# Layer 2's transposes and layer 3's RMS factors by transfers, bias rows and loop blocks added by transfers from GpSimd

## The chip, the cores and the metric

The kernel runs on one core of one Trainium2 chip. The metric is the device time of one execution in microseconds (us). The engines are named as the profile names them: PE is TensorE (PEld its weight loads), DVE is VectorE, ACT is ScalarE, POOL is GpSimd, SP is SyncE, which here only issues transfers.

## What is computed

Thirty-two graphs of 512 nodes pass through four layers. Each graph has node features x (512 x 256) and an adjacency adj (512 x 512), all in float32, and each layer is followed by a residual sum and a layer norm:

```python
# layer 0: GIN
h = (1.0 + eps) * x + adj @ x
x = layernorm(x + (relu(h @ W1 + b1) @ W2 + b2))            # hidden 512
# layer 1: GCN
h = adj @ (x @ W.T + b)
x = layernorm(x + where(h > 0, h, alpha * h))
# layer 2: a layer norm of its own, then a graph convolution
h = layer_norm(x, gamma, beta)
x = layernorm(x + (x + relu((adj @ h) @ W_rel + b_rel + h @ W_root)))
# layer 3: GIN with an RMS norm
h = (eps * x + adj @ x) @ W1 + b1                            # hidden 1024
x = layernorm(x + (silu(h * rsqrt(mean(h * h) + 1e-6) * w) @ W2 + b2))
```

## The kernel before

**Products by seven.** Every large product is a Strassen-Winograd scheme (`seven`, lines 583 to 599): operands are cut into 2 x 2 blocks, sums of blocks are formed on VectorE (`left_sums`, `right_sums`), and seven block products stand for eight. Weights get their sums once, the adjacency gets its sums once per graph (`Adjacency.sums`, line 650), features at each use. `aggregate` (line 685) forms adj @ x transposed, with features on partitions; `dense_feat` (line 725) multiplies by a weight and stays feature-major; `dense_add` (line 768) returns to token-major and adds into a tile that already holds the residual; `dense_tok` (line 713) is layer 1's plain product. A graph has 106 matmuls of 256 columns, 112 of 128 columns and 12 transposes on TensorE. A float32 matmul leaves two records in the trace, a transpose one.

**Where the change touches.**
- *Loops.* The factors (1 + eps) of layer 0 and eps of layer 3 lie on the diagonal of the adjacency. Four diagonal blocks, in the adjacency's two halves and in two of its sums (`self.loops`, line 655), are saved before layer 0 (`kept`, four transfers within SBUF, lines 659 to 665), get a scaled identity added on VectorE (`with_loops`, line 671: four additions of 128x256), are restored after layer 0 (`restore`, line 667: four transfers) and get another identity added after layer 2 (line 951).
- *Bias rows.* `plus_row` (line 874) adds a 256-wide bias to a 512 x 256 tile in four additions on GpSimd, in layer 0 (line 901) and layer 3 (line 958). The evictions of `dense_add` then add to that tile.
- *Layer 2's transposes.* h is token-major and is needed feature-major too: eight TensorE transposes of 128 x 128 into two PSUM banks and two copies out (lines 938 to 943).
- *RMS factors.* Layer 3 squares h, sums it over features (`column_sums`, line 793: one transposing reduction and three small additions on VectorE leave 32 partitions x 4 sums for each quarter), scales the sums in four small instructions, takes the power -1/2 on GpSimd (`inv_sqrt`, line 513, 128 x 4), and spreads each token's factor to all partitions by four transposes of a broadcast column into PSUM (lines 971 to 977). VectorE multiplies hT by that PSUM bank (line 981), ScalarE takes silu, VectorE forms sums, and the second dense product follows.

**What sets the order.** The whole program is written out by a planner (`Plan`, lines 191 to 403). Every operation is recorded with its engine (some may go to ScalarE or VectorE), a cost from formulas (lines 36 to 80), and what it must wait for. `order` (line 317) then plays all engines forward, each with one queue in order, and picks on each the ready operation with the lowest rank; ranks come from the graph's number times a period plus how much TensorE work of that graph lies ahead. `RULES` (line 95) lists the sets of period and pace tried; the one that ends first in the planner's reckoning is written out. Four graphs may be in flight (`FLIGHT`, line 444); they share 36 SBUF tiles of 128 x 1024 (`rooms`), 12 small tiles and 8 PSUM banks, and a graph further back must leave some free (`spare`). All transfers are issued by SP in that order (`move`, line 276), reckoned at 0.45 us of SP (`ISSUE`), 1.5 us, the bytes and 0.35 us to land; eight are in flight at most (`LANES`). GpSimd has the bias additions and the powers. All instructions come from one helper line (L266), transfers from L280.

Of the kernel before, what the change touches and what calls it, by code (L numbers as in the profile page):

```python
# [26 lines left out]


def in_psum(x):
    return isinstance(x, Part) and x.room.pool.psum  # L30
# [35 lines left out]
def gpsimd_time(n):  # L66
    return 0.15 + n * 0.0024, 0.05


# [6 lines left out]
ISSUE, ADVANCE, AFTER, LANES = 0.45, 1.5, 0.35, 8  # L76
# [18 lines left out]
RULES = [(50, 2, last, near) for last in (12, 20) for near in (0, 0.5, 1)]  # L95


class Pool:


    def __init__(self, tiles, grain, spare, psum):
        self.tiles, self.grain, self.spare, self.psum = tiles, grain, spare, psum
        self.clear()

    def clear(self):
        self.rooms = [None] * len(self.tiles)

    def free(self):

        return sorted(  # L110
            (0.0 if r is None else r.until, i)
            for i, r in enumerate(self.rooms)
            if r is None or not r.left
        )


class Room:


    def __init__(self, pool):  # L120
        self.pool = pool
        self.uses = 0
        self.clear()

    def clear(self):
        self.index = None
        self.left = self.uses
        self.until = 0.0


class Part:
# [34 lines left out]
    def place(self):  # L166
        v = self.room.pool.tiles[self.room.index]
        for step in self.steps:
            v = step(v)
        return v  # L170
# [3 lines left out]
class Op:  # L174

    graph: int
    rank: tuple
    ways: dict  # L180
    port: set
# [9 lines left out]
class Plan:  # L191
# [10 lines left out]
    def grains(self, x):  # L202
        part = isinstance(x, Part)
# [4 lines left out]
        for step, n in dims[:-1]:  # L208
            starts = [s + step * i for s in starts for i in range(n)] if step else starts
        step, n = dims[-1]  # L210
        return {
            (key, g)
            for s in starts
            for g in range(s // grain, (s + step * (n - 1)) // grain + 1)
        }

    def add(self, ways, out, ins, ordered=None, port=(), kbytes=0):
        me = len(self.ops)
        op = Op(self.graph, (self.graph, me), ways, port, "scalar" in ways, kbytes)
        self.ops.append(op)  # L220
        before, results = set(), set()
        writes = self.grains(out) if out is not None else set()
# [22 lines left out]
    def do(self, out, *ways, ordered=None, scrap=None):  # L245
# [3 lines left out]
        port = set()  # L249
        for e, method, _, args, kw in ways:  # L250
            tiles = [x for x in (*args, *kw.values()) if isinstance(x, (bass.AP, Part))]
            ins += tiles
            if e == "gpsimd" and kw.get("op") != ALU.pow or e == "vector" and not (
                method.startswith("bn_") or any(in_psum(x) for x in tiles)
            ):
                port.add(e)

        def issue(engine, method, args, kw):
# [14 lines left out]
            out, ins, ordered, port,  # L273
        )

    def move(self, out, src, kbytes, inward=True):


        def issue():
            self.nc.sync.dma_start(*(x.place() if isinstance(x, Part) else x for x in (out, src)))  # L280

        self.add(
            {"sync": ((ISSUE, ADVANCE + wire_time(kbytes) + AFTER), issue)},
            out if inward else None, [src] if isinstance(src, Part) else [], kbytes=kbytes,
        )
# [31 lines left out]
    def order(self, period, pace, last, near):  # L317
# [15 lines left out]
        oldest, port, wire, lanes = 0, 0.0, 0.0, [0.0] * LANES  # L333
        can_start = {i for i, n in enumerate(behind) if not n}
        done = []
        while can_start:
# [4 lines left out]
            def rooms_free(op):  # L341

                count = {}
                for r in op.rooms:
                    if r.index is None:
                        count[r.pool] = count.get(r.pool, 0) + 1
                at = 0.0
                for pool, n in count.items():
                    if pool not in room_at:
                        room_at[pool] = pool.free()  # L350
                    n += pool.spare[min(op.graph - oldest, len(pool.spare) - 1)]
                    if op.graph - oldest >= self.flight or n > len(room_at[pool]):
                        return None
                    at = max(at, room_at[pool][n - 1][0])
# [3 lines left out]
            for i in can_start:  # L358
# [4 lines left out]
                if op.kbytes:  # L363
                    wait = max(wait, lanes[0])
                at = {
                    e: max(free[e], wait, ready[i][e], port if e in op.port else 0.0)
                    for e in op.ways
                }
                way = min(at, key=lambda e: at[e] + sum(op.ways[e][0]) + (YIELD if op.yields and e == "vector" else 0.0))
# [11 lines left out]
            if op.kbytes:  # L381
                wire = max(wire, t + ADVANCE) + wire_time(op.kbytes)
                end = wire + AFTER
                lanes = [*lanes[1:], end]
            if engine in op.port:
                port = end
            for r in op.rooms:
                if r.index is None:
                    r.index = r.pool.free()[0][1]
                    r.pool.rooms[r.index] = r  # L390
# [16 lines left out]
def tile_gnn_stack(ctx: ExitStack, tc: tile.TileContext, a: dict, out: bass.AP):  # L407
# [36 lines left out]
    FLIGHT, ROOMS, SMALL = 4, 36, 12  # L444
# [3 lines left out]
    psum = ctx.enter_context(tc.tile_pool(name="psum", bufs=1, space=bass.MemoryType.PSUM))  # L448
    plan = Plan(nc, FLIGHT)

    def pool(kind, name, n, size, grain, spare):
        return Pool(
            [kind.tile([P, size], F32, tag=f"{name}{i}", name=f"{name}{i}") for i in range(n)],
            grain, spare, kind is psum,
# [3 lines left out]
    rooms = pool(work, "room", ROOMS, NC * D, P, (0, 4, 6, 8))  # L458
# [5 lines left out]

    def gpsimd(method, n, *args, **kw):
        return "gpsimd", method, gpsimd_time(n), args, kw
# [22 lines left out]
    def both(method, o, x, y, engines):  # L489
        plan.do(o, *(e(method, span(o), x, y) for e in engines))  # L490

    def add(o, x, y, *engines):
        both("tensor_add", o, x, y, engines or (vector,))

    def sub(o, x, y, *engines):
        both("tensor_sub", o, x, y, engines or (vector,))

    def mul(o, x, y):
        both("tensor_mul", o, x, y, (vector,))
# [10 lines left out]
    def carry(o, x):  # L510
        plan.move(o, x, P * span(o) / 256)

    def inv_sqrt(o, x):
        n = span(o)
        plan.do(
            o, ("gpsimd", "tensor_tensor", power_time(n), (x, mhalf[:, 0:n]), dict(op=ALU.pow))
# [3 lines left out]
    def room(*shape):  # L520
        return Part(Room(rooms)).shaped(*shape)

# [54 lines left out]
    mhalf = constant("mhalf", [P, 2 * NC])  # L577
# [56 lines left out]
    class Adjacency:  # L634
# [15 lines left out]
        def sums(self):  # L650
# [8 lines left out]
            kept = room(4, HC, P)  # L659
            self.plain = [kept[:, i] for i in range(4)]  # L660
            for d, o in zip(self.plain, self.loops):
                if plan.graph:
                    carry(d, o)
                else:
                    copy(d, o)

        def restore(self):
            for d, o in zip(self.plain, self.loops):
                carry(o, d)

        def with_loops(self, loop):
            for d, o in zip(self.plain, self.loops):
                add(o, d, loop.unsqueeze(1).to_broadcast(list(o.shape)), vector)

        def row_sums(self):

            rows = room(N)
# [79 lines left out]
    def dense_sums(upper, lower):  # L757
# [3 lines left out]
        for pairs in zip(upper, lower):  # L761
            blocks = [x[:, :, j * TH : (j + 1) * TH] for x in pairs for j in range(2)]
            sums = right_sums(*blocks, [room(2, TH) for _ in range(3)], blocks[1])
# [29 lines left out]
    def column_sums(t, put):  # L793
# [3 lines left out]
        few = small(16)  # L797
# [7 lines left out]
        for q in range(1, P // Q):  # L805
            add(few[0:Q], few[0:Q], few[q * Q : (q + 1) * Q])
        for q in range(P // Q):
            put(slice(q * Q, (q + 1) * Q), few[0:Q, q :: P // Q])
# [64 lines left out]

    def plus_row(x, r):

        for c in range(NC):
            add(x[:, c, :], x[:, c, :], r, gpsimd)
# [31 lines left out]
    def layer1(x, adjacency):  # L909
# [4 lines left out]
        column_sums(rows, lambda p, sums: ts(rs[p], sums, 1.0, None, ALU.mult))  # L914
# [20 lines left out]
    def layer2(h, xx, u, adjacency):  # L935

        aT = aggregate(h, adjacency)
        hT = Wide(DC)
        for j in range(DC):
            ps = bank(N)  # L940
            for c in range(NC):
# [144 lines left out]
```

## Time and profile before

| | |
|---|---|
| median of 3 runs | 2364.99 us (2363.84 to 2365.42) |
| profiled execution: time, span, mean granted clock | 2366.02 us, 2364.2 us, 0.997 |
| PE: busy, instructions | 2330.0 us (99%), 14362 |
| DVE: busy, instructions | 2138.4 us (90%), 5485 |
| ACT: busy, instructions | 1570.1 us (66%), 3994 |
| POOL: busy, instructions | 407.7 us (17%), 422 |
| additions of loop blocks on DVE | 256 x 416 ns = 103.9 us |
| additions of bias rows on POOL | 256 x 769 ns = 194.6 us |
| powers on POOL, 4 and 8 columns | 128 x 1243 ns, 32 x 1672 ns |
| transfers within SBUF | 252 of 128 KB, 2.2 us from issue to landing |
| packets of SP's queue | 103280, 14.5% of 16 engines' span |

How it is read: *busy* is the union of an engine's records and the share is of the span. In a group's line, "line engine op out<-in" come first, then shapes and count, then busy time, the mean of one, and the idle time of that engine just before with what ended most of it. In a table by stretches, each line has the stretch, its length, then each engine's busy time with the number of instructions in brackets, then TensorE's granted clock (1.00 is full), the busy share of the transfer engines and GB/s. Matmuls are pipelined, so their records overlap: the mean of one record is longer than the time from one start to the next. The last chain is followed back from the last instruction, at each step to what released it.

### The profile page before, as it was taken

The numbers are of one execution on the slowest core, as the hardware profiler recorded it, in microseconds if no ns is written. First come the engines' busy times: TensorE is split into PE (matmuls) and PEld (weight loads), VectorE is DVE, ScalarE is ACT, GpSimd is POOL, SyncE is SP. The second block draws the span as 40 slices with busy tenths as digits, with TensorE's granted clock in tenths as the row PEclk, the third lists the DMA queues.
The fourth block names the chain that finished last, engine by engine and source line by source line (L and its number), as shares of the span: only waits on it lengthen the run. The fifth ranks groups of instructions, "written<-read, shape, count | busy, mean of one in ns | idle before, by whom it ended". The sixth has DMA issues, their size and how long they took to land.

```text
span 2364.2 us, 40948 instructions
## 1 busy us (share of the span) xinstructions
PE 2330.0 (99%) x14362; PEld 2135.4 (90%) x14362; DVE 2138.4 (90%) x5485; ACT 1570.1 (66%) x3994; POOL 407.7 (17%) x422
## 2 busy tenths in 40 slices
PE   8999999999999999999999999999999999989997
PEld 7899989999999999999999999999999989978997
DVE  6899989999999999999999999999999999988997
ACT  3767666667666676766676666776666766565764
POOL 1112111111121121111111211111111112111111
PEclk9999999999999999999999999999999999999999
DMA  7001110111110111101111101111011111011000
GB/s 218 12 8 54 50 54 12 52 50 51 53 35 30 50 54 50 54 14 50 50 52 52 44 20 50 54 50 54 14 50 50 52 52 46 23 52 48 10 10 28
DMA packets 103487, 107.25 MB, mean 45 GB/s; under 512 B 10865, under 2 KB 78193, under 8 KB 103281
## 3 DMA queue, kind: packets, MB, share of 16 engines
q1 hardware_dynamic: 103280, 104.64, 14.5%
q8 instruction: 113, 1.85, 0.3%
q14 instruction: 94, 0.76, 0.1%
HBM read 54.80 MB, written 16.78 MB: 30 GB/s over the span
## 4 chain that ended last, share of the span: by engine, by line
PE 91%; DVE 4%; DMA 2%; ACT 1%; issue 1%; SPq 0%; POOL 0%; POOLq 0%; ACTq 0%; DVEq 0%
PE ps L266 91%; DVE room L266 3%; ACT room L266 1%; DVE few L266 1%; DMA room<-in_x_dram 1%; ACT scrap L266 1%; DMA room<-room 1%; SPq L280 0%; DMA L_gnn_eps<-in_L_gnn_eps_dram 0%; DMA room<-in_adj_dram 0%; POOL few L266 0%; ACT L266 0%; POOLq L1082 0%; DVE L_gnn_W L266 0%; DVE A L266 0%
## 5 line engine op out<-in xcount | busy, mean ns | idle before, releaser
L266 PE MATMUL ps<-room,room 128*128 128x256 f32 x3584 | 911.9, 380 | 9.8 <-DMA room<-in_x_dram 5.8
L266 DVE TENSOR_TENSOR room<-ps,room 128x256 f32<-128x256 f32 (+1 forms) x1344 | 629.6, 475 | 149.3 <-PE ps L266 122.6
L266 PEld LDWEIGHTS ps<-room,room 128*128 128x128 f32 x3584 | 650.1, 191 | 88.8 <-issue 7.1
L266 DVE TENSOR_TENSOR room<-room,room 128x512 f32<-128x512 f32 (+1 forms) x1120 | 640.6, 585 | 9.9 <-ACT room L266 3.1
L266 PE MATMUL ps<-L_gnn_W,room 128*128 128x128 f32 (+1 forms) x3584 | 622.7, 291 | 7.2 <-ACT room L266 4.9
L266 PEld LDWEIGHTS ps<-L_gnn_W,room 128*128 128x128 f32 x3584 | 525.3, 192 | 31.1 <-ACT room L266 7.2
L266 PE MATMUL ps<-A,room 128*128 128x128 f32 x3072 | 489.2, 276 | 1.8 <-ACT room L266 1.1
L266 PEld LDWEIGHTS ps<-A,room 128*128 128x128 f32 x3072 | 434.8, 192 | 15.8 <-ACT room L266 1.3
L266 PE MATMUL ps<-room,L_gnn_W 128*128 128x256 f32 x1536 | 424.6, 380 | 1.0 <-DVE room L266 0.9
L266 ACT ACTIVATE room<-ps,L_gnn_b_c 128x256 f32<-128x256 f32 x768 | 318.2, 472 | 157.2 <-PE ps L266 157.0
L266 POOL TENSOR_TENSOR few<-few,mhalf 128x4 f32<-128x4 f32 (+1 forms) x160 | 212.5, 1329 | 1211.0 <-DVE few L266 1208.5
L266 ACT ACTIVATE room<-ps 128x256 f32<-128x256 f32 (+1 forms) x546 | 215.0, 407 | 298.5 <-PE ps L266 294.7
L266 ACT ACTIVATE room<-room,few 128x256 f32<-128x256 f32 x624 | 341.0, 603 | 107.0 <-DVE few L266 103.7
L266 DVE TENSOR_TENSOR room<-room 128x256 f32<-128x256 f32 (+1 forms) x640 | 330.4, 518 | 18.0 <-DMA room<-in_adj_dram 5.7
L266 POOL TENSOR_TENSOR room<-room,L_gnn_b 128x256 f32<-128x256 f32 x256 | 194.6, 769 | 739.6 <-PE ps L266 519.0
L266 PE MATMUL ps<-room,A 128*128 128x256 f32 x1152 | 319.2, 380 | 3.0 <-ACT room L266 3.0
L266 PEld LDWEIGHTS ps<-room,L_gnn_W 128*128 128x128 f32 x1536 | 279.7, 191 | 33.1 <-DVE room L266 2.2
L266 ACT ACTIVATE room<-room 128x1024 f32<-128x1024 f32 (+2 forms) x260 | 245.8, 946 | 18.1 <-DVE room L266 16.5
L266 ACT ACTIVATE room<-room,L_gnn_rms_weight_c 128x512 f32<-128x512 f32 x256 | 179.7, 718 | 111.3 <-DVE room L266 108.2
L266 PEld LDWEIGHTS ps<-room,A 128*128 128x128 f32 x1152 | 206.5, 191 | 27.1 <-ACT room L266 4.2
L266 ACT ACTIVATE scrap<-room 128x256 f32<-128x256 f32 x384 | 157.2, 411 | 74.3 <-DVE room L266 63.1
L266 ACT ACTIVATE scrap<-room,few 128x256 f32<-128x256 f32 x384 | 190.7, 498 | 18.1 <-DVE few L266 16.3
(53 smaller groups left out, 1453.4 us busy)
## 6 DMA issues: line engine op xcount, KB each, us to landing
room<-in_adj_dram SPq DMA_DIRECT2D x128, 256.0 KB, 5.0
room<-room SPq DMA_DIRECT2D x252, 128.0 KB, 2.2
room<-in_x_dram SPq DMA_DIRECT2D x32, 512.0 KB, 6.0
out_dram<-room SPq DMA_DIRECT2D x32, 512.0 KB, 3.0
L_gnn_W<-in_L_gnn_W_dram SPq DMA_DIRECT2D x2, 1024.0 KB, 8.5
L_gnn_W<-in_L_gnn_W_dram SPq DMA_DIRECT2D x2, 512.0 KB, 8.1
L_gnn_b<-in_L_gnn_b_dram SPq DMA_DIRECT2D x3, 128.0 KB, 5.0
L_gnn_W_rel<-in_L_gnn_W_rel_dram SPq DMA_DIRECT2D x1, 256.0 KB, 7.2
```

What stands on the lines that cost most here:

```text
L266: getattr(getattr(self.nc, engine), method)(to, *(put(x) for x in args), **kw)
```

## The change

- Layer 2 (`turned`): but for the first and the last graph, VectorE transposes h in 32 x 32 squares (two instructions of 128 x 512), and SP moves the squares to their places in sixteen transfers (32 partitions, 8 x 32 elements each) within SBUF.
- Layer 3 (`everywhere`): but for the first and the last graph, the scaled sums stay on 32 partitions (32 x 16), the power is taken there, one transfer writes the 512 factors to a line in DRAM in single elements, and another reads the line back to all partitions. The multiplications of hT read SBUF instead of PSUM.
- Loop blocks (`with_loops`): but for the first and the last graph, the identity is added by four transfers from GpSimd that add to their destination, in layer 0 and after layer 2. From graph 1 on only the two blocks of the sums are saved, to DRAM; the other two are restored from adj itself, in 128 x 128 blocks (two transfers each).
- Bias rows (`plus_row`): in all graphs one adding transfer from GpSimd of 128 x 1024.
- The planner gets a cost of 1.2 us for an issue on GpSimd, no longer keeps VectorE and GpSimd apart, and tracks partitions by quarters of 32; rooms may be split in halves (`short`); five graphs may be in flight, with other spare rooms and other rules.

A count of the program's transfers: 463 issued by SP before; 1003 by SP and 304 by GpSimd after. TensorE transposes: 384 before, 24 after.

```diff
-ISSUE, ADVANCE, AFTER, LANES = 0.45, 1.5, 0.35, 8
+ISSUE, ADVANCE, AFTER, LANES = dict(sync=0.45, gpsimd=1.2), 1.5, 0.35, 8
...
-RULES = [(50, 2, last, near) for last in (12, 20) for near in (0, 0.5, 1)]
+RULES = [(p, c, last, near) for p, c in ((36, 2), (45, 2.5)) for last in (12, 20) for near in (0.25, 0.5)]
...
-    FLIGHT, ROOMS, SMALL = 4, 36, 12
+    FLIGHT, ROOMS, SMALL = 5, 36, 11
...
+    lines = cycle([memory.tile([N], F32, tag=f"line{i}", name=f"line{i}") for i in range(FLIGHT)])
...
+    def alone():
+
+        return plan.graph in (0, B - 1)
...
-    rooms = pool(work, "room", ROOMS, NC * D, P, (0, 4, 6, 8))
+    rooms = pool(work, "room", ROOMS, NC * D, P, (0, 2, 4, 4))
...
+    def pour(o, x):
+
+        plan.move(o, x, P * span(o) / 256, engine="gpsimd", outof=(o, x), accum_op=ALU.add)
...
-            kept = room(4, HC, P)
-            self.plain = [kept[:, i] for i in range(4)]
-            for d, o in zip(self.plain, self.loops):
-                if plan.graph:
-                    carry(d, o)
+            if plan.graph:
+                self.kept = next(diagonals)
+                for i in (2, 3):
+                    d = self.kept[:, i - 2]
+                    name = f"{self.kept.tensor.name}{i}"
+                    plan.move(d, self.loops[i], P * HC * P / 256, into=name)
...
+                elif i < 2:
+                    for k in range(HC):
+                        c = i * HC + k
+                        block = a["adj"][plan.graph][:, c, c * P : (c + 1) * P]
+                        plan.move(self.loops[i][:, k], block, P * P / 256)
...
         def with_loops(self, loop):
-            for d, o in zip(self.plain, self.loops):
-                add(o, d, loop.unsqueeze(1).to_broadcast(list(o.shape)), vector)
+            for o in self.loops:
+                loops = loop.unsqueeze(1).to_broadcast(list(o.shape))
+                if alone():
+                    add(o, o, loops)
+                else:
+                    pour(o, loops)
...
+    def turned(h):
+
+        hT = Wide(DC)
+        if alone():
+            for k in range(DC):
+                ps = bank(N)
+                for c in range(NC):
+                    flip(ps[:, c * P : (c + 1) * P], h[:, c, k * P : (k + 1) * P])
+                copy(hT.chunk(k), ps)
+        else:
+            squares = Wide(DC)
+            for k in range(DC):
+                o = squares.chunk(k)
+                plan.do(o, vector("transpose", N, h[:, :, k * P : (k + 1) * P]))
+            places = [slice(q * Q, (q + 1) * Q) for q in range(P // Q)]
+            to, of = (
+                x.pair(0).then(lambda v: v.rearrange("p k (c i) -> p (k c) i", i=P))
+                for x in (hT, squares)
+            )
+            for p in places:
+                for q in places:
+                    carry(to[p, :, q], of[q, :, p])
+        return hT
+
+    def everywhere(sums, ops):
+
+        if alone():
...
+        else:
+            few = small(2, N // Q)
+            ve, power = few[0:Q, 0, :], few[0:Q, 1, :]
+            ts(ve, sums, *ops)
+            inv_sqrt(power, ve)
+            o, line = short(N), next(lines)
+            plan.move(line.rearrange("(m i) -> i m", i=Q), power, N / 256, into=line.tensor.name)
+            plan.move(o, line.partition_broadcast(P), P * N / 256, outof=[line.tensor.name])
+        return o
+
     def plus_row(x, r):
 
-        for c in range(NC):
-            add(x[:, c, :], x[:, c, :], r, gpsimd)
+        pour(x, r.unsqueeze(1).to_broadcast([P, NC, D]))
...
-        hT = Wide(DC)
-        for j in range(DC):
-            ps = bank(N)
-            for c in range(NC):
-                flip(ps[:, c * P : (c + 1) * P], h[:, c, j * P : (j + 1) * P])
-            copy(hT.chunk(j), ps)
+        hT = turned(h)
...
-        pr = bank(N)
-        for c in range(NC):
-            flip(pr[:, c * P : (c + 1) * P], rstd[:, c : c + 1].spread(P, P))
+        pr = everywhere(column_sums(acc), (1.0 / HID3, RMS_EPS, ALU.mult, ALU.add))
```

## The prediction

> **What bounds the kernel now.** I read the page first: part 1 for the shares, part 2 for where in time they lie, part 4 for the chain that ended last.
>
> ```profile
> PE 2330.0 (99%) x14362; PEld 2135.4 (90%) x14362; DVE 2138.4 (90%) x5485; ACT 1570.1 (66%) x3994; POOL 407.7 (17%) x422
> PE 91%; DVE 4%; DMA 2%; ACT 1%; issue 1%; SPq 0%; POOL 0%; POOLq 0%; ACTq 0%; DVEq 0%
> ```
>
> TensorE is busy 99% of the span and holds 91% of the last chain. VectorE at 90% is the next bound. Since a busy TensorE need not be one at its peak, I then asked for the busy time by stretch.
>
> ```profile
> 0.00:25.00 25.00, 21.24 (x82) 17.34 (x82) 13.97 (x37) 8.26 (x18) 3.57 (x10) 1.00 0.84 255
> 25.00:50.00 25.00, 20.65 (x110) 17.67 (x111) 18.44 (x53) 10.17 (x30) 3.94 (x5) 0.93 0.85 260
> ...
> 1000.00:1500.00 500.00, 500.00 (x3108) 460.53 (x3108) 460.18 (x1183) 340.92 (x870) 89.59 (x91) 1.00 0.14 42
> ...
> 2050.00:2100.00 50.00, 45.99 (x247) 39.90 (x246) 40.98 (x115) 30.41 (x79) 4.35 (x4) 1.00 0.17 53
> ...
> 2340.00:2364.00 24.00, 14.87 (x112) 14.39 (x112) 15.03 (x39) 8.72 (x15) 2.01 (x2) 0.82 0.11 45
> ```
>
> The second number is the stretch, the third TensorE's busy time. From 200 to 2050 us TensorE has no gap (its waits from 200 to 2000 us add to 0.5 us). The missing 34 us lie in the first 200 us, where x and adj are awaited, and in the last 315 us. So in the middle a TensorE instruction taken out is time taken out, as long as nothing new makes it wait. What an instruction takes there is read from start to start in the timeline, because records overlap:
>
> ```profile
> 1062.86 0.49 PE L266 MATMUL ps<-ident,room 128*128 128x128 f32 x3
> 1063.19 1.03 PE L266 MATMUL ps<-room,room 128*128 128x256 f32 x4
> 1064.06 0.49 PE L266 MATMUL ps<-ident,room 128*128 128x128 f32 x3
> ...
> 1068.08 0.60 PE L266 MATMUL ps<-ident,few 128*128 128x128 f32 x4
> 1068.51 0.60 PE L266 MATMUL ps<-room,A 128*128 128x256 f32 x2
> ```
>
> Three transposes take 1063.19 - 1062.86 = 0.33 us and four take 0.43 us: 0.108 us each, not the 0.27 us of one record. A 256-column matmul (two records) takes (1064.06 - 1063.19) / 2 = 0.43 us, a 128-column one in the same way 0.2236 us.
>
> **What the Trainium skill says.** "TensorE: Matmul & The Clock Gate", Part 4: PE-mode transpose, gives about 275 ns for a transpose inside a kernel. The record here shows 273 ns, but the slot is 108 ns, and I use the slot. "DMA: Bandwidth & Descriptors", SWDGE vs HWDGE vs iDMA, says that accumulating transfers can only be issued from GpSimd, whose cores write the descriptors in software. The kernel before has none, so its trace neither confirms a price nor shows one. The same page, Anatomy of one DMA, gives a fixed cost of about 2 us. The SBUF-to-SBUF moves here land in 2.2 us, which agrees. "SBUF — State Buffer", Who interferes with whom: a VectorE instruction with two SBUF inputs and a GpSimd instruction that reads SBUF exclude each other. The 256 GpSimd additions of 0.77 us go, but the trace shows little of that: VectorE's 128x512 additions take 0.696 us with two SBUF inputs and 0.685 us with one in PSUM.
>
> **The change part by part.**
>
> *TensorE.* In 30 of 32 graphs the 8 transposes of layer 2 and the 4 of the RMS factors go. The written order confirms it: 384 transposes before, 24 after, everything else the same. 30 x 12 x 0.108 = 38.9 us. As a check, all slots before add to 2315.5 us (3405 x 0.4325 + 3584 x 0.2236 + 384 x 0.108), after to 2276.6 us.
>
> *VectorE and ScalarE.* Out: 240 additions of loop blocks (0.416 us each, 100 us), 90 small scalings net (0.16 us, 14 us), 26 copies out of PSUM that go to ScalarE (11 us). In: 60 square transposes of 512 elements. The nearest row is the transposing reduce, 128x512 at 0.707 us, so 42 us; bounds 0.4 us (a pass at twice the rate) and 1.4 us (half the rate), 24 to 84 us. VectorE goes from 2138 to about 2055 us, 90% of the new span: no new bound even at the upper end. ScalarE loses 60 copies of 0.6 us. None of this is on the path while TensorE is full: 0 us.
>
> *GpSimd.* Out: 256 additions of 0.77 us. In: 304 adding transfers (30 x 8 loop blocks and 32 x 2 bias rows). The trace has no DMA issue on POOL. SP's take 0.35 to 0.55 us; the skill ("DMA: Bandwidth & Descriptors", Specifications) has about 1 us to the first byte on this path, which is the value I take, with 0.4 and 3 us as ends. 10 us a graph beside five powers of 1.2 to 2.5 us fills a quarter of the 71 us that a graph lasts. The powers queue behind these issues; VectorE and ScalarE wait for them.
>
> *SP and the DMA engines.* A graph goes from 14 issues to 32, at 0.45 us some 14 us of 71. Packets grow by about 220,000 (30 x (16 x 256 squares + 8 x 256 loops + 2 x 512 rows + 640 for factors), less the saved copies). At the 53 ns that a packet cost before (14.5% of 16 engines over 103,280 packets) that is 31% more, some 45% in all: room enough.
>
> *Waits that are added, and their cover.* In TensorE slots, for a graph in the middle:
> - Layer 2's squares: 16 issues (7.2 us) and a landing (2.2 us), instead of 0.9 us of transposes and a copy. From layer 1's last matmul to layer 2's first dense one lie 47.5 us of other matmuls in the new order, 26.0 in the old. Covered, with over 10 us to spare. SP's other moves queue for those 7 us.
> - RMS factors: from the last matmul of layer 3's first dense part to the first of its second lie 23.4 us in the new order, 15.2 in the old, which was enough without a wait. The chain loses flips and three small scalings (1.2 us), gains 1.3 us of power (16 columns for 4; 0.107 us a column from 1.243 and 1.672 us at 4 and 8) and two transfers in a row, of 4-byte pieces to DRAM and back to all partitions. 2.2 us is the least for each, 4.4 us (the landing of the broadcast b_rel row) the most: 4.4 to 8.8 us against 8.2 us of extra cover. I take 6 us: covered, just. Behind it on VectorE stand the multiplications of hT and every later eviction.
> - Loop blocks of layer 3: about 21 us between layer 2's last aggregate matmul and layer 3's first; one transfer needs 3 to 6. Bias rows: over 16 us. Covered.
> - Loop blocks of layer 0: four adding transfers stand in a row on POOL right after the sums. The planner that wrote the order counts on 1.2 us of POOL for each and 2.2 us to land (its constants are in the code), 7 us in all, and puts the first readers about 2 us behind the landing that it expects. This is the thinnest cover.
>
> *Head and tail.* Five graphs may be in flight for four. In slots a graph now spreads over 283 us for 210, so four overlap where three did. The last four graphs end 36, 19, 7 and 0 us of slots before the end (72, 28, 13 and 0 before), so TensorE has more than one graph's work for longer. The last 315 us had 23 us of gaps; I take 8 us of them off, and 2 us of the head's 11. The ends are 0 and 20 us. The first and last graph keep the old way for transposes and loops.
>
> *Sum.* 2364.2 - 38.9 - 10 + 5 (30 graphs x 0.15 us for the thin covers) = 2320.3 us of span. The profiled execution was 2366.0 us, 1.8 more than its span, and 1.0 above the median of the runs: 2364.99 - 43.9 = 2321 us.
>
> **The rivals.**
> - *Part of it is given back.* The two transfers of the RMS factors take 9 us rather than 6; VectorE stands at the multiplications and TensorE runs dry for about 1 us a graph: 30 us back, 2350 us. For it: the chain is serial, 4-byte pieces are new here, DRAM is in between. Against it: 8.2 us of extra cover, and no chain of the old order made TensorE wait. 2335 to 2360 us.
> - *Slower: adding transfers hold POOL.* If one costs 2.4 us of POOL instead of 1.2, the fourth loop block of layer 0 is 4 x 1.2 = 4.8 us late, 2.8 us beyond its cover, and TensorE, which takes its matmuls in order, stands for that in every graph: 30 x 2.8 = 84 us against 44 gained, 2405 us. It decides from about 2.1 us an issue (30 x 1.5 us uses up the gain). For it: descriptors by software, 256 to 512 pieces each, and no price in this trace. Against it: POOL has 83% of its time free and the loads are early.
> - *Nothing.* TensorE is full but VectorE, at 90% too, sets the pace through its order; the slots that go turn into waits: 2363 us. Against it: VectorE loses twice as much work (83 us) as TensorE.
> - That the transposes are not gone is excluded by the written order.
>
> **How the numbers follow.** 0.48 for the covered case, 2300 to 2334 us (all of the tail's 20 us, or none of it and 5 us of waits more); 0.22 for the part given back, 2335 to 2360; 0.06 for within 0.2% (4.7 us, about what a measurement of this kernel can tell from no change); 0.24 for slower, 2370 to 2430 and above. That is faster 0.70, same 0.06, slower 0.24. The likeliest is 2320 us. From 2300 to 2380 us I leave out most of the slower case and little else, 0.2. The likeliest case's own range is 2300 to 2334.
>
> **What would show it.** Right: TensorE busy about 2290 us and full from 200 us on; flips x24; TensorE waits on DMA of rooms under 5 us; SP at about 1000 issues; POOL issues near 1 us. Wrong: TensorE waits of 1 us or more that come back every 71 us, released by a DMA from a line (RMS factors) or by adding transfers (loop blocks); VectorE waiting for the broadcast room for over 1 us a graph; POOL's issues over 2 us; a square transpose far above 0.7 us.

## The result and the profile after

The changed kernel takes 2592.56 us (median of four runs, 2591.97 to 2593.03) against 2364.76 us (2363.84 to 2365.42): a ratio of 1.0963, 95% interval 1.0944 to 1.0982. The prediction said 2320 us, with 2300 to 2380 as its range. It is 227.8 us slower, where 44 us less were forecast.

The page of the changed kernel, TensorE's line of part 1 and the engines of the chain that ended last:

```profile
PE 2384.1 (92%) x14002; PEld 2144.8 (83%) x14002; DVE 2027.0 (78%) x5195; ACT 1537.5 (59%) x3954; POOL 646.3 (25%) x470
PE 43%; DVE 25%; DMA 16%; SPq 8%; POOL 3%; issue 3%; ACT 2%; DVEq 0%; POOLq 0%; ACTq 0%
```

The 360 transposes are gone, yet TensorE is busy 54 us longer, and its share of the chain has fallen from 91% to 43%. Most of the rest of the chain is VectorE, transfers and SP: no engine is full any more. The busy time by stretch shows it in the middle of the kernel:

```profile
1000.00:1500.00 500.00, 463.00 (x2746) 417.63 (x2745) 386.36 (x986) 299.38 (x768) 128.34 (x93) 0.97 0.38 76
```

Where TensorE had no gap before, it has 37 us of gaps in 500 and a granted clock of 0.97. The waits by engine (engine, what it waits to read or overwrite, who releases it: us in all, times, longest) name the place:

```profile
PEld ps L283 <- DVE room L283: 136.9, 85, 7.7
PE ps L283 <- DVE room L283: 115.7, 55, 7.3
PE ps L283 <- ACT room L283: 63.9, 28, 5.4
DVE room L283 <- DMA room<-line: 114.7, 27, 7.9
DVE room L283 <- DMA room<-room: 84.4, 26, 4.6
DVE room L283 <- DMA room<-diagonal: 53.7, 11, 6.9
```

TensorE waits for VectorE, and less for ScalarE. (A weight load and its matmul often wait for the same thing, so the PEld and PE lines are not added.) VectorE waits for the RMS factors (a room from a line) 27 times in 30 graphs, for layer 2's squares (a room from a room) 26 times, and for restored loop blocks (a room from a diagonal) 11 times. The waits of SP's queue show that it stands too:

```profile
SPq L298 <- POOL few L283: 232.5, 30, 49.9
SPq L298 <- DMA line<-few: 184.4, 30, 7.5
```

In each graph SP first stands until the power is there, then until the line is written; what is queued on SP behind these stands too. The list of transfers (last numbers: KB each, us from issue to landing) and GpSimd's groups by shape give what the new operations take:

```profile
room<-L_gnn_b POOLq DMA_DIRECT2D x64, 512.0 KB, 5.5
room<-loop POOLq DMA_DIRECT2D x240, 128.0 KB, 3.5
room<-room SPq DMA_DIRECT2D x480, 32.0 KB, 1.9
room<-line SPq DMA_DIRECT2D x30, 256.0 KB, 3.6
line<-few SPq DMA_DIRECT2D x30, 2.0 KB, 6.9
```

```profile
L298 POOL DMA_DIRECT2D room<-loop x240 | 291.8, 1474 | 786.6 <-PE ps L283 709.6 <-DVE room L283 51.7 <-DMA diagonal<-room 20.1
L283 POOL TENSOR_TENSOR few<-few,mhalf 32x16 f32<-32x16 f32 x30 | 101.1, 3369 | 116.6 <-DVE few L283 116.6
```

The smallest transfer of these five, 2 KB in 512 single elements, is the slowest: 6.9 us. The power of 16 columns takes 3.37 us.

**How a graph goes now.** The chain of waits, read in order of time from 1030 to 1125 us (start, length, what), is a loop:

```profile
1035.51 2.90 POOL few L283
1038.43 7.84 DMA line<-few
...
1046.41 3.30 DMA room<-line
...
1049.74 1.03 DVE room L283 x2
...
1050.82 20.25 PE ps L283 x96
...
1076.66 0.59 SPq L298
...
1087.11 1.91 DMA room<-room
...
1089.70 1.03 DVE room L283 x2
...
1090.77 17.77 PE ps L283 x110
...
1118.07 2.90 POOL few L283
...
1120.99 7.56 DMA line<-few
```

Power, line, broadcast, VectorE's multiplications, 20 us of TensorE, a layer norm, sixteen issues on SP (10.5 us with what lies between them), landing, 18 us of TensorE, VectorE's sums, and then the power of the next graph, 82.6 us after the first. TensorE is on this loop for 38 us of 83. In the rest it lives on what other graphs offer, and in this loop that runs out twice, for 5.58 us at 1045 and for 1.66 us at 1089. The timeline shows the first time:

```profile
1039.17 0.38 SPq L298 DMA_DIRECT2D room<-diagonal  x1
...
1046.41 0.32 SPq L298 DMA_DIRECT2D room<-line  x1
1046.80 0.43 DVE L283 TENSOR_TENSOR room<-room 128x256 f32<-128x256 f32 x1 [4.55 <-DMA room<-diagonal]
```

```profile
1050.82 1.22 PE L283 MATMUL ps<-L_gnn_W,room 128*128 128x256 f32 x2 [5.58 <-DVE room L283]
```

VectorE has stood 4.55 us for the restored block, works for a moment, then stands for the broadcast; TensorE has stood 5.58 us (the bracket). The wait for the block belongs to the line too. SP issued the block 0.74 us after the line, and it landed only with it (list of transfers, 1036 to 1050 us):

```profile
room<-diagonal SPq DMA_DIRECT2D x1, 128.0 KB, 7.6
line<-few SPq DMA_DIRECT2D x1, 2.0 KB, 7.8
```

Eleven of the 62 restored blocks were issued while a line was being written. They landed in 7.3 to 8.6 us, the other 51 in a median of 2.3 us, and VectorE's 11 waits for such blocks, 53.7 us in all, are for these eleven. With the line in whole pieces, in an experiment below, this wait is gone from the list.

The pause costs more than its own length. The busy time in short stretches around that pause (TensorE's busy time comes third, its granted clock third from the end):

```profile
1045.00:1050.80 5.80, 0.23 (x2) 0.00 (x0) 2.90 (x10) 0.34 (x1) 1.01 (x1) 0.94 0.26 53
1050.80:1055.00 4.20, 4.18 (x10) 3.38 (x11) 2.80 (x6) 3.56 (x7) 0.00 (x0) 0.50 0.00 0
1055.00:1060.00 5.00, 5.00 (x24) 4.28 (x23) 4.05 (x9) 2.68 (x6) 1.33 (x1) 0.81 0.05 7
1060.00:1065.00 5.00, 5.00 (x32) 4.62 (x31) 4.99 (x13) 4.17 (x16) 0.00 (x0) 1.00 0.87 153
```

After the pause TensorE runs at half its clock for about 6 us: from 1050.82 to 1056.94 it does seven 256-column matmuls, which at 0.4325 us are 3.0 us of work. So this pause costs 5.6 + 3.1 = 8.7 us. The Trainium skill ("TensorE: Matmul & The Clock Gate", Part 1: The HAM clock gate) says that an idle window of about 3.4 us halves the clock. The trace agrees in the main: 0.50 after pauses of 5.58 and, a loop later, 5.83 us, and no loss after those of 1.66 and 1.92 us. Near 3.4 us the length alone does not decide. Two pauses of the same length, and the stretch after each:

```profile
1295.55 0.54 PE L283 MATMUL ps<-L_gnn_W,room 128*128 128x128 f32 x2 [3.66 <-ACT room L283]
1372.82 0.49 PE L283 MATMUL ps<-L_gnn_W,room 128*128 128x128 f32 x2 [3.67 <-ACT room L283]
```

```profile
1295.90:1299.30 3.40, 3.40 (x13) 2.84 (x12) 3.40 (x8) 2.86 (x5) 0.00 (x0) 0.50 0.46 71
1372.80:1376.90 4.10, 4.08 (x24) 3.70 (x24) 4.10 (x9) 3.23 (x6) 0.00 (x0) 1.00 0.41 62
```

The whole loss divides the same way. The span, 2590.2, less 2276.6 of slots, less the 48.7 us that were not slots before, leaves 265 us, 8.8 a graph. TensorE stands 206.1 us for 34.2 before, 5.7 us more a graph; and it is busy 107.5 us beyond its slots for 14.5 before, 3.1 us more a graph, about what half clock costs after a pause such as the one above.

### The profile page after: what moved, and what is told of

Its sections match the earlier page's. It is cut to its first block, busy times and chain, and to the rows that moved or that the text cites. A ratio compares the mean times of both kernels' runs of the same rounds, so it can differ in the third digit from the quotient of the medians.

```text
span 2590.2 us, 41342 instructions
## 1 busy us (share of the span) xinstructions
PE 2384.1 (92%) x14002; PEld 2144.8 (83%) x14002; DVE 2027.0 (78%) x5195; ACT 1537.5 (59%) x3954; POOL 646.3 (25%) x470
## 4 chain that ended last, share of the span: by engine, by line
PE 43%; DVE 25%; DMA 16%; SPq 8%; POOL 3%; issue 3%; ACT 2%; DVEq 0%; POOLq 0%; ACTq 0%
PE ps L283 43%; DVE room L283 22%; SPq L298 8%; DMA line<-few 7%; DMA room<-line 4%; POOL few L283 3%; DVE few L283 3%; DMA room<-room 2%; ACT room L283 2%; DMA room<-diagonal 1%; DMA room<-in_adj_dram 1%; DMA diagonal<-room 0%; DMA room<-in_x_dram 0%; DMA L_gnn_eps<-in_L_gnn_eps_dram 0%; DMA room<-loop 0%
## 5 line engine op out<-in xcount | busy, mean ns | idle before, releaser
L283 PE MATMUL ps<-room,room 128*128 128x256 f32 x3584 | 979.0, 391 | 45.7 <-DVE room L283 24.9
L283 DVE TENSOR_TENSOR room<-room,room 128x512 f32<-128x512 f32 (+1 forms) x1360 | 773.3, 594 | 124.0 <-DMA room<-line 114.7
L283 PE MATMUL ps<-L_gnn_W,room 128*128 128x128 f32 (+1 forms) x3584 | 686.6, 303 | 112.7 <-DVE room L283 60.4
L283 PEld LDWEIGHTS ps<-L_gnn_W,room 128*128 128x128 f32 x3584 | 604.2, 199 | 184.3 <-DVE room L283 67.8
L283 POOL TENSOR_TENSOR few<-few,mhalf 128x4 f32<-128x4 f32 (+2 forms) x160 | 272.5, 1706 | 874.9 <-DVE few L283 852.4
L298 POOL DMA_DIRECT2D room<-loop x240 | 291.8, 1474 | 786.6 <-PE ps L283 709.6
L283 PE MATMUL ps<-A,room 128*128 128x128 f32 x3072 | 471.0, 277 | 5.7 <-DVE room L283 5.7
L283 DVE TENSOR_TENSOR room<-room 128x256 f32<-128x256 f32 (+1 forms) x640 | 311.5, 497 | 163.7 <-DMA room<-room 84.4
L283 PEld LDWEIGHTS ps<-room,L_gnn_W 128*128 128x128 f32 x1536 | 261.2, 191 | 53.6 <-DVE room L283 34.6
L283 ACT ACTIVATE room<-ps 128x256 f32<-128x256 f32 (+1 forms) x512 | 187.4, 375 | 189.9 <-PE ps L283 188.4
```

The costliest lines, as they stand in the source:

```text
L283: getattr(getattr(self.nc, engine), method)(to, *(put(x) for x in args), **kw)
L298: getattr(self.nc, engine).dma_start(to, of, **kw)
```

## The experiments

A measured time is that of one run (the kernel before took 2364.87 to 2366.35 us beside them), unless a range is given. T is the theory held when a run was sent in, R its rival. The first T was: transfers take longer than the order was written for, first of all the RMS factors' way through DRAM and then the squares; VectorE stands, TensorE runs dry. Its rivals were the adding transfers, and the new order with five graphs in flight. One caution holds for all: the planner writes out a new order for each edit, so two runs differ by their orders too, not only by the edit.

### Which part it is

**RMS factors the old way** (transposes of broadcast columns, in all graphs).

```diff
     def everywhere(sums, ops):
...
-        if alone():
+        if True:
```

> The changed kernel with the RMS factors spread in the old way (four small scalings, a power of 4 columns, four TensorE transposes); squares and adding transfers stay. Theory (VectorE stands before transfers that take longer than the order was written for, first of all the line to DRAM and back): the 115 us of VectorE waits for the line go and with them SP's 184 us behind it; 2400 to 2480 us. Rival (the adding transfers on GpSimd are what costs): 2560 us or more. Rival (five graphs in flight and the new order cost by themselves): 2560 us or more.

Measured 2419.08 us. 173.5 of the 227.8 us are gone. What is left shows in the waits:

```profile
DVE room L283 <- DMA room<-room: 129.1, 25, 6.1
```

**Layer 2's transposes the old way** (the same edit in `turned`).

> The changed kernel with layer 2's transposes in the old way on TensorE; line and adding transfers stay. Theory: VectorE's 84 us of waits for squares go, and SP's 16 issues of 0.65 us no longer stand before other moves; the line stays; 2470 to 2540 us. Rival (adding transfers): 2560 us or more.

Measured 2590.92 us: a miss, and inside the range of the rival, the adding transfers, which the next two runs rule out. The squares' waits are gone, and the line's have grown from 114.7 us to

```profile
DVE room L283 <- DMA room<-line: 152.5, 29, 7.7
```

so taking out the second wait of the loop freed nothing while the first was there.

**Both the old way**; the adding transfers and the new planner stay.

> The changed kernel with both sets of transposes in the old way, so that only the adding transfers and the new planner settings stay. Theory (line and squares are the whole loss): 2345 to 2385 us, TensorE full in the middle. Rival (adding transfers, or five graphs in flight, are the loss): 2500 us or more.

Measured 2387.29 us, 2 us above T's range and far below its rival's.

**Everything the old way**: the loop blocks added on VectorE and the bias rows on GpSimd as well. Only the new planner and its settings stay.

```diff
         def with_loops(self, loop):
...
-                if alone():
+                if True:
...
-        pour(x, r.unsqueeze(1).to_broadcast([P, NC, D]))
+        for c in range(NC):
+            plan.do(x[:, c, :], ("gpsimd", "tensor_add", (0.15 + D * 0.0024, 0.05), (x[:, c, :], r), {}))
```

> The changed kernel's planner (five graphs in flight, split rooms, new rules, VectorE and GpSimd no longer kept apart) with every part done in the old way: both sets of transposes on TensorE, loop blocks added on VectorE, bias rows on GpSimd. If the adding transfers are what makes the kernel that has only them 22 us slower than before: 2355 to 2370 us. If the new order itself is what costs: 2380 us or more.

Measured 2426.78 us. Two things follow. The adding transfers are not the harm: in this planner the kernel is 39 us faster with them. And the new planner's order by itself costs 62 us on unchanged work. The prediction had no such rival; the first experiments had one, at a much larger size.

### Is it the length of the transfers, or an order that counts them too short?

**The line in whole pieces.** One more 32 x 32 transpose on VectorE turns the powers, so that the line is written in 16 pieces of 128 bytes; the planner's costs of transfers stay.

```diff
+            plan.do(turn, vector("transpose", Q, both))
...
-            plan.move(line.rearrange("(m i) -> i m", i=Q), power, N / 256, into=line.tensor.name)
+            plan.move(line.rearrange("(m i) -> i m", i=Q), turn[0 : N // Q], N / 256, into=line.tensor.name)
```

> The changed kernel with one edit: the 32 x 16 factors are turned on VectorE once more (one 32 x 32 square), so that the line in DRAM is written in 16 pieces of 128 bytes instead of 512 of 4. The planner's costs are not touched. Theory (the 4-byte pieces make the write land in 6.9 us): it lands in 2.5 us or less, and 2420 to 2500 us. Rival (any write to DRAM that is read at once takes that long): it lands in 5 us or more, 2560 us or more.

Measured 2450.74 us. The transfer and the wait for it, from the list of transfers and the waits:

```profile
line<-few SPq DMA_DIRECT2D x30, 2.0 KB, 1.3
```

```profile
DVE room L283 <- DMA room<-line: 1.0, 2, 0.7
```

The same bytes land in 1.3 us instead of 6.9, and the wait is gone, with 142 us of the loss. The planner's prices are still those of the change.

**Only the RMS factors' cost put right in the planner**; the instructions are those of the change.

```diff
-    return 0.37 + n * 0.158, 0.04
+    return 0.4 + n * 0.2, 0.04
...
-            plan.move(..., power, N / 256, into=line.tensor.name)
-            plan.move(o, line.partition_broadcast(P), P * N / 256, outof=[line.tensor.name])
+            plan.move(..., power, N / 256, into=line.tensor.name, late=5.0)
+            plan.move(o, line.partition_broadcast(P), P * N / 256, outof=[line.tensor.name], late=1.1)
```

> The changed kernel, with the planner given the measured cost of the RMS route alone (line write 5.0 us later, read 1.1 us later, powers 0.4 us + 0.2 us a column); squares and adding transfers stay priced as in the change. Theory (the line is the mis-sized cost that decides): 2375 to 2430 us. Rival (the price of the squares on SP and of the adding transfers matters as much): 2480 us or more.

Measured 2394.14 us, and 198 us of the loss are gone. The line is about as slow as before, but it is hardly waited for:

```profile
line<-few SPq DMA_DIRECT2D x30, 2.0 KB, 6.3
```

```profile
DVE room L285 <- DMA room<-line: 1.0, 2, 0.6
```

**All costs put right**: also 0.65 us of SP for a square, 1.4 us of GpSimd for an adding transfer, and 1.3 or 2.3 us more for it to land.

> The changed kernel, every part of it, but the planner is given what the trace measured: line to DRAM lands 5.0 us later, line back 1.1 us later, squares hold SP 0.65 us each, adding transfers hold POOL 1.4 us and land 1.3 or 2.3 us later, powers 0.4 us + 0.2 us a column. Theory (costs mis-sized by the order, which is fixed, so that VectorE stands in line): most of the loss goes, 2300 to 2370 us. Rival (the chain through transfers is too long for five graphs, whatever the order): 2450 us or more.

Measured 2376.32 us, 216 us less than the changed kernel, though 6 us above what T gave. The transfers are as slow as before; they are only reckoned with. VectorE waits 1.7 us in all for lines and 53.7 us for squares.

**Both**: whole pieces, all costs right, and more combinations in `RULES` (periods 36, 42, 50, 60, each with pace 2 and 2.5).

> Line in 128-byte pieces as in the run before, and every other transfer priced as the trace measured it; more combinations of the planner's rules are tried. Theory: the best of these kernels, 2325 to 2370 us, with TensorE waits for VectorE under 60 us in all. Rival (waits come from how close the order is written, whatever the prices): 2376 us or more.

Measured 2362.93 us: level with the kernel before, though 38.9 us of slots have gone. Lines are hardly waited for any more; what is left are many short waits of TensorE, more than the 60 us that T allowed:

```profile
PEld ps L285 <- DVE room L285: 64.8, 137, 3.2
PE ps L285 <- DVE room L285: 21.8, 49, 3.0
```

### What the new planner's own order costs

The waits pointed to the hand-over from VectorE to TensorE. The old planner let a VectorE operation between SBUF tiles start only after the end of the one before, its 0.085 us of tail too, since it kept VectorE and GpSimd's additions apart (`port`). The change drops that. In the changed work GpSimd has no such additions, so there the rule acts through VectorE alone. T was now: without it the planner counts VectorE too fast, and places matmuls where their operands come late.

```diff
-                at = {e: max(free[e], wait, ready[i][e]) for e in op.ways}
+                at = {e: max(free[e], wait, ready[i][e], port if e in op.port else 0.0) for e in op.ways}
...
+            if engine in op.port:
+                port = end
```

**The rule put back, on the version of 2362.93 us; on the version with the line in single elements, all costs right and more periods; and on the old parts.**

> As the run with the line in whole pieces and every measured cost in the planner (2362.93 us), and in the planner alone the old rule comes back that an operation of VectorE between tiles of SBUF starts only when the one before it has ended, its 0.085 us of tail too. No instruction is added or taken away. Theory T (the planner of the change counts VectorE too fast, so its order has multiplications stand for results of VectorE that come late): 2310 to 2345 us, and TensorE's waits for VectorE fall well below the 65 + 22 us of that run. Rival R (five graphs in flight, fewer spare rooms and the new rules make the poorer order, or there is no more to be had): 2355 to 2385 us, those waits unchanged.

> The change with its own line of 4-byte pieces, every measured cost in the planner (that was 2376.32 us), wider rules, and the old rule of VectorE back in the planner. T: 2320 to 2360 us; R: 2365 to 2390 us. Against the run beside it, it tells what the line in 4-byte pieces costs once it is known to the planner: T expects 10 us or less.

> The new planner with every part of the work done the old way (that was 2426.78 us, 62 us over the kernel before), and the old rule of VectorE back in it. T: 2360 to 2385 us, the loss gone. R: 2405 to 2430 us.

**And the old settings instead of the rule**, on the old parts.

```diff
-RULES = [(p, c, last, near) for p, c in ((36, 2), (45, 2.5)) for last in (12, 20) for near in (0.25, 0.5)]
+RULES = [(50, 2, last, near) for last in (12, 20) for near in (0, 0.5, 1)]
...
-    FLIGHT, ROOMS, SMALL = 5, 36, 11
+    FLIGHT, ROOMS, SMALL = 4, 36, 12
...
-    rooms = pool(work, "room", ROOMS, NC * D, P, (0, 2, 4, 4))
+    rooms = pool(work, "room", ROOMS, NC * D, P, (0, 4, 6, 8))
```

> The new planner with every part the old way and without the old rule of VectorE, but with the settings of before: four graphs in flight, 12 small tiles, spare rooms 0, 4, 6, 8 and the old periods. T: 2405 to 2430 us, as with the new settings. R: 2360 to 2385 us.

Measured 2344.64, 2354.98, 2383.25 and 2445.87 us. The first three lie in the ranges of T, near their upper ends, and the line in single elements cost 10.3 us where T gave 10 or less. The fourth lies above both ranges: the settings are not what costs, as R had it, but T's size was missed too. The rule takes 18 us off the changed work and 44 us off the old parts (2426.78 to 2383.25). In the old parts it also keeps GpSimd's bias additions off VectorE's operations (they take 830 ns without it and 759 ns with it), so not all of the 44 us need be slack; the old settings without it take nothing off (they add 19). In the first of the four TensorE's waits for VectorE fall from 65 and 22 us to 32 and 21. **Old parts, rule and old settings together**, and **four graphs in flight for the changed work**, closed the account:

> The new planner with every part the old way, the old settings and the old rule of VectorE: all that is left of the change is the planner's rewritten book-keeping. If the settings cost the 18 us that the run with the new settings and the old rule lay over the kernel before: 2360 to 2370 us. If something else of the new planner does: 2378 to 2388 us.

> The version of 2344.64 us with four graphs in flight in place of five and spare rooms of 0, 4, 6, 8 in place of 0, 2, 4, 4. If the fifth graph and the rooms are cover for the new transfers: 2355 to 2390 us. If the new settings are a loss for any work: 2325 to 2340 us.

Measured 2369.05 and 2451.5 us. The first is within 3 us of the kernel before: with the rule, the old settings are the better ones for the old work, by 14 us, and nothing else of the new planner costs much. The second is 107 us over the version that it was made from, well above what either theory gave: in this planner the changed work needs the fifth graph and the new spare rooms.

### Is there more of the same?

**More slack**, in two ways, on the version of 2344.64 us: every VectorE operation counted 0.03 us longer, or 0.4 us in place of 0.25 us between a result and the matmul that reads it.

```diff
-HAND = dict(tensor=0.25, vector=0.13, scalar=0.13, gpsimd=0.18, sync=0.2)
+HAND = dict(tensor=0.4, vector=0.13, scalar=0.13, gpsimd=0.18, sync=0.2)
```

> The version of 2344.64 us with each VectorE operation counted 0.03 us longer in the planner. If its order is still too tight between VectorE and TensorE: 2320 to 2340 us. If not: 2342 to 2365 us, since VectorE is then counted as nearly full.

> The version of 2344.64 us with 0.4 us in place of 0.25 us in the planner between the end of any result and the multiplication that reads it. If its order is still too tight there: 2320 to 2340 us. If not: 2342 to 2360 us.

Measured 2358.7 and 2321.83 us. The first way is a loss of 14 us. The reason expected for that, that VectorE is then nearly full in the reckoning, is not shown. The second, only where TensorE reads, is worth 23 us. It was measured again with several runs, beside the same with the change's own line of single elements:

> The version of 2321.83 us again, in five rounds for an interval: 2318 to 2326 us, 1.6 to 2.0% under the kernel before.

> Every part of the change as it is, its line of 4-byte pieces too; in the planner alone the measured costs, the old rule of VectorE and 0.4 us before a multiplication. If the order was all that was wrong: 2318 to 2330 us. If the line in 4-byte pieces still costs as much as between the two runs without the slack (2344.64 and 2354.98 us): 2330 to 2340 us. If its waits come back whatever the order: over 2350 us.

Measured 2324.87 us (2321.9 to 2328.55), ratio 0.9828 with an interval of 0.9814 to 0.9841; and 2346.08 us (2344.9 to 2353.85), ratio 0.9927, 0.9913 to 0.9941. Both beat both kernels. In the first of them the middle is full again, and the waits for VectorE and for lines are down to 10 us or less:

```profile
1000.00:1500.00 500.00, 500.00 (x3076) 461.17 (x3076) 451.92 (x1156) 339.38 (x876) 155.56 (x106) 1.00 0.41 82
```

```profile
PEld ps L294 <- DVE room L294: 10.3, 14, 1.4
PE ps L294 <- DVE room L294: 5.9, 8, 1.2
DVE room L294 <- DMA room<-line: 2.7, 2, 2.0
```

The second lies between two of the expected bands. Its TensorE waits for VectorE 30.6 us at weight loads and 19.0 us at matmuls, and VectorE for no line, so the 21 us between the two are not waits for the line itself. Whether the longer way of the factors tightens the order elsewhere, or the planner merely chose a poorer order, stays open.

## Why the prediction was wrong, point by point

- *TensorE: 38.9 us of slots go.* Right, and given back only when the order lets it. In the best version TensorE is full from 1000 to 1500 us, and it gains 2366.24 - 2324.87 = 41.4 us. The premise "a TensorE instruction taken out is time taken out, as long as nothing new makes it wait" held; its condition did not.
- *RMS factors: "I take 6 us: covered, just".* This is the step that failed. Write and read take 6.9 + 3.6 = 10.5 us, beyond even my upper end of 8.8, which was itself over the 8.2 us of cover. I had bounded the write by its bytes and by other transfers' landings, and took 2.2 to 4.4 us for 512 pieces of 4 bytes. The Trainium skill ("DMA: Bandwidth & Descriptors", Specifications) gives 512 bytes as the least transfer for full rate. That alone would not have told the price: pieces of 128 bytes lie below it too, and they land in 1.3 us. The two runs show that it is the pieces that count, not the bytes, though not what in them costs.

  The power added 3.37 us for a reckoned 2.5 (1.243 and 1.3 more). By my own sum the chain grew by 10.5 + 1.3 + 0.8 - 1.2 = 11.4 us against 8.2 us of extra cover: 3 us late, in an order that cannot move. The order itself was written for less than I took: by the constants in its code 1.9 us for the write and 2.5 us for the read, 6.1 us short together, and the run with these two and the power put right (2394.14) shows what that was worth. I had named what stands behind it on VectorE, but not what a pause of over 5 us does to TensorE's clock, 3.1 us on top of 5.6, nor that a loop block issued behind the write lands late with it.
- *Squares: "covered, with over 10 us to spare".* Sized too low, 16 x 0.65 us on SP for 16 x 0.45, and wrong as a separate item: VectorE waited for them 26 times. The cover of 47.5 us was counted in TensorE slots of an order without waits. That other graphs' matmuls are used up once the loop of factors, sums and squares runs on its own time, and then no longer cover, is how I read the chain; no run tests it alone. Undoing the squares alone gave nothing (2590.92); undoing them after the factors took 32 us more (2419.08 to 2387.29). They were second.
- *SP.* I counted its issues (14 us a graph), not its standing: 417 us at the power and the line, where transfers of other graphs queue. What this standing costs by itself, no run shows.
- *Adding transfers.* Mis-sized a little, right in effect: 1.33 to 1.47 us of GpSimd for the 1 us taken, far from the 2.1 us at which the rival decides. TensorE's matmuls wait 5.5 us in all for loop blocks. That the kernel came out slower, as this rival had it, was luck: its mechanism did not show.
- *VectorE.* 2027 us for a reckoned 2055, 0.692 us a transpose for 0.7: right (2055 us would have been 89% of the forecast span, not 90%).
- *The planner.* This is a second term that was wrong: I put the new order at nothing but 5 us of thin covers, and gave no reason. On old work the new planner costs 62 us. Removing `port` had looked free because the operations that it kept apart were gone; it had also given each VectorE operation between SBUF tiles up to 0.085 us of slack. That the rule is worth 18 us on the changed work is shown by the run with it back; that it works through this slack, rather than through the other orders that come with it, is supported by the run with 0.4 us before matmuls and not more than that, since the run with slack on all of VectorE went the other way.
- *Head and tail: 10 us off.* Too much: in the best version 2323.0 - 2276.6 = 46.4 us of the span are not slots, for 48.7 before.
- *"Part given back"* had the right mechanism, TensorE running dry behind the factors, at the wrong size: 1 us a graph, where it was 8.8. I let the transfers be 3 us longer than the 6 I took, and did not follow the pause into the clock and into the next graph.

Taken in one line, each run against the one before it: 2592.6 (the change), 2394.1 (the RMS factors priced right), 2376.3 (all transfers priced right), 2355.0 (the rule of VectorE, and more periods), 2346.1 (0.4 us before matmuls), 2324.9 us (the line in whole pieces). Without touching an instruction, other prices and rules in the planner take away 246 of these 268 us; and making the write short had taken 142 us with the old prices. The loss lay in the gap between what the order reckoned and what the transfers took, and each side closed most of it.

## What to carry to other kernels

When a kernel's order is fixed ahead by reckoned costs, a new operation can cost more by what the reckoning gets wrong, once per repetition, than by what it takes: here 6.1 us too short in the reckoning and 8.8 us lost a graph. Price it by a measured run and put that into the planner before judging the operation. A transfer in single elements was slow here for its pieces and not its bytes, and it held up the transfer behind it; turning the data first, which made whole rows, took that away. Slack that looks like a left-over rule may be what keeps a full engine full: here it was worth most where the full engine reads.

## What the runs showed of the hardware

- 512 pieces of 4 bytes to DRAM land in 6.9 us, the same 2 KB in 16 pieces of 128 bytes in 1.3 us.
- A transfer of 128 KB issued on the same queue during that write landed in 7.3 to 8.6 us, otherwise in 2.3 us.
- A pause of TensorE of 5.6 us cost 3.1 us more at half clock; pauses below 2 us cost only themselves. Of two pauses of 3.66 and 3.67 us, one was followed by 3.4 us of half clock and the other by none.
- An adding transfer holds GpSimd for 1.3 to 1.5 us and lands in 3.5 us (128 KB) or 5.5 us (512 KB); in the middle of the best version TensorE stayed full beside them.
- A power on GpSimd took longer with more columns, not with more elements: 128 x 4 took 1.06 us (1.24 us in the kernel before), 128 x 8 took 2.12 us, and 32 x 16, with as many elements as the first, took 3.37 us.
- The issue of a 32-partition square holds SP for about 0.61 us (0.65 us from start to start), where the two other issues shown above take 0.32 and 0.38 us.
